# Row sums spread by VectorE transposes, the order of work in tables, and four LayerNorm tiles off TensorE

## The chip, the cores and the metric

The kernel runs on one core of one Trainium2 chip. A core has five engines with a queue of instructions each: TensorE (PE in the profile; its weight loads are the row PEld), VectorE (DVE), ScalarE (ACT), GpSimd (POOL) and SyncE (SP), which here only issues DMAs. Each queue runs in order; engines wait for one another by semaphores. The metric is the time of one execution on the device, in microseconds.

## The reference, cut to what matters

Eight sequences of 256 tokens with 512 features pass through four layers, all in float32: attention, a feed-forward layer, attention with other weights, and the same feed-forward layer again.

```python
x = x + _L0_attn_a_ref(_layernorm(x, axis=-1), w_qkv, w_o)
x = x + _L0_ffn_ref(_layernorm(x, axis=-1), gate_w, base_w, base_b, lora_A, lora_B)
x = x + _L0_attn_b_ref(_layernorm(x, axis=-1), wq, wk, wv, wo)
x = x + _L0_ffn_ref(_layernorm(x, axis=-1), gate_w, base_w, base_b, lora_A, lora_B)
```

Attention has 32 query heads on 8 key and value heads of 16 features, rotary embedding, a causal mask and a softmax. The feed-forward layer is a 512x512 projection with bias, plus low-rank terms of the two best of eight experts, weighted by a softmax over their two gate values.

## The kernel before, in words

The work is 16 units: a sequence in its first attention and feed-forward layer, or the same sequence in its second pair. Units 0 to 3 and 8 to 11 are first passes, 4 to 7 and 12 to 15 the second. A unit has two tiles of 128 tokens (t = 0, 1). For each tile a LayerNorm gives `xn` (statistics L631 to L635 and L638 on VectorE, a power L637 on GpSimd, the scaling L640 on ScalarE), four TensorE transposes (L647) turn it, and ScalarE copies the result out of PSUM (L654) into `xnT` or `yT`, features on partitions.

An attention unit then projects keys (L675), values (L686) and queries (L746), and applies the rotary embedding on VectorE and GpSimd from tables in `rtab`; the cosines and sines come by two DMAs on ScalarE's queue and two VectorE copies (L602). Scores are computed twice. The first pass (L801; groups s10 to s14) is copied to a `big` buffer (L816), masked by GpSimd (L832) and reduced to row maxima (L846), which a TensorE transpose (L855), a copy (L858) and DMAs put into spare rows of `q`. The second pass (L887; s20 to s24) gives transposed scores with the maximum taken off, which ScalarE exponentiates (L902) and GpSimd masks (L913). The value matmuls (L932; pv) sum them against `vp`, which also has 16 columns of ones for each group of four heads. So their PSUM result holds outputs and row sums interleaved: for half s, rows 32i to 32i+31 hold 16 rows of outputs and 16 equal rows of sums.

ScalarE copies this result to `e`, 128x2x512 (L947). Two DMAs gather the sums to `sums` (L952), VectorE takes the reciprocal of 128x32 (L955), two DMAs write it to DRAM as `recd` (L959), and one reads it back, each row repeated 16 times, as `rec` (L963). COPY_PREDICATED (L966) merges the two halves of `e`, overwriting sums, and a multiplication (L970) scales by `rec`. Then come the output projection (L978) and the addition to x (L985). The feed-forward layer has the gate and low-rank matmul (L999), the gate's small steps on VectorE (L1018 to L1044), a transpose (L1049), the 512x512 matmul (L1063), the low-rank matmul (L1069) and the addition (L1079).

Everything is registered with `plan.add(engine, cost, tag, function, reads, writes, ...)` before anything is issued: 2,955 operations. A planner, `Plan.schedule`, then walks through time with its own costs. For each engine it starts the ready operation with the lowest rank from the list `RANKS`, provided that its buffers are free; it lends PSUM banks and pooled buffers as it goes. The order in which it started them is the order of issue, so each engine's queue has it. TensorE's steps have a kind: full (128-row matmuls and transposes), score (L801, L887) and value (L932). SyncE has every load and store but the two tables; at most eight DMAs are under way.

The steps of the start that matter later: SyncE loads the first tile of sequence 0, its second tile, then the two halves of the first query weights (copied into place by VectorE, L556). The first full projection is L746 on both tiles.

Of the kernel before, what the change touches and what calls it, by code (L numbers as in the profile page):

```python
# [26 lines left out]
CHANGE = {"full": 0.08, "score": 0.16, "value": 0.13}  # L27
APART = 0.07
WINDOW = 3.4
SPLIT = 16  # L30
FIXED = 1.65
QUEUED = 8
# [3 lines left out]
RANKS = """  # L36
0 65 400 0 585 195 130 455 260 680 716 752 788 390 1870 955 2165 3555 325 3195 1105 1655 2615 2760
715 3645 1030 1795 2830 520 650 1240 1520 2905 1725 2255 2685 1280 1338 1680 1738 0 100 200 300 400
500 615 637 676 761 335 396 406 430 491 521 609 680 413 474 484 508 567 597 736 810 1676 1945 1852
2084 2150 2187 2277 2410 2345 2346 2373 2444 2566 2525 2657 2607 876 1407 1609 1674 1796 2515 1053  # L40
1230 1432 1497 1514 2150 3485 3130 2800 2922 3015 3259 3392 3532 3313 3435 3528 3779 3942 4228 4060
3741 3956 3863 4105 4216 4388 4514 4124 4411 4246 4565 4644 4743 4414 4779 4536 4977 5056 5142 5024
5235 5331 5266 5434 5644 5740 5675 5913 6035 6128 6237 6349 6203 6325 6418 6588 6797 6371 6511 6604
6527 6805 6712 6728 6991 6898 7100 7212 7105 7262 7371 7436 7710 7789 7854 8059 7571 8439 8920 9311
6914 7339 7550 7659 7724 8405 8450 8515 8735 8025 9203 9383 9931 9372 9654 9664 9893 9992 10057
10329 10400 11025 10882 11003 11037 11089 11072 11161 11301 11212 11456 11585 11672 11771 10472
12243 12372 10005 10066 10076 10428 10598 10683 10836 10907 11281 11560 11789 11823 11952 11858
11988 12039 12059 12079 12088 12347 12454 11075 12632 12824 1133 1194 1204 1228 1287 1317 1584 1655
824 885 895 919 978 1008 1630 1705 2038 2307 2214 2425 2723 2760 2642 3325 3260 2669 2811 2882 3271
3180 3312 3221 2897 3090 3353 3292 3525 3652 2446 2623 2872 2937 3005 3132 3870 3940 4927 5049 5142  # L50
5262 5522 5713 5229 5351 5444 5655 5766 6163 5995 5623 5745 5838 6004 6115 6522 6354 7487 7643 7736
7845 7924 8090 7237 7457 7364 7566 7645 7804 6620 6697 6728 6793 8328 8574 8605 8670 7781 7996 7903
8105 8371 10039 10254 10161 10480 10689 10978 11202 11109 11463 11585 11678 10375 10590 10497 11152
11436 11694 11859 11968 12033 12233 12405 12340 12610 12168 12990 13178 13600 11834 12009 12166
12470 12275 12670 12780 12715 13010 12698 13390 13590 13965 13829 13890 13900 14611 14932 14967
15090 15208 15067 15814 15935 15969 16021 16004 16057 16108 16128 16148 16157 16720 16763 15426
17193 17306 14026 14087 14097 14480 14539 14845 14947 15039 14933 16624 16745 16836 16947 16871
16983 17054 17034 17074 17083 17374 17411 16829 17479 17620 1055 1116 1126 1150 1211 1241 2400 2475
2794 2855 2865 2953 3059 3108 3267 3362 3472 4031 3648 4149 4302 4339 4327 4215 4280 4354 4423 4494
4872 4913 4679 4629 4573 4750 5025 4964 5135 5395 3838 4221 4449 4682 4723 4850 5594 5529 8080 8202  # L60
8295 9084 9217 9433 8177 8481 8388 8664 8846 9142 8974 8533 8655 8748 9782 10051 10832 10304 8823
9078 8985 9545 9624 9710 9286 9408 9501 9703 9945 10083 11451 11491 11702 11572 11439 11476 11507
11637 12141 12268 12361 12470 12582 12535 12750 12657 12859 13479 14993 15115 15258 14480 14752
14609 15329 15451 15544 15653 15765 14037 14248 14422 14357 14839 14884 14949 15154 14867 15534
17664 18055 16007 16198 16355 16529 16464 16737 16782 16847 17052 16765 17445 19336 19790 18116
18177 18187 18238 18362 18530 18943 19014 18655 19702 19823 19912 20106 20264 20213 20435 20308
20590 20599 22493 22549 20029 22630 23042 19851 20168 20178 20234 20295 20325 20681 20765 20415
20837 21048 21228 21309 21263 21493 21661 21681 21729 22387 22602 22720 21779 22754 22903 1898 1959
1969 1993 2052 2134 3410 3621 2998 3072 3082 4053 4289 4339 4511 4729 7589 7878 7987 8105 8311 8348
8344 8171 8236 10024 8525 8775 8853 8894 8935 9171 5052 5446 5648 5934 5877 8217 8356 8630 8848 8913  # L70
8957 9418 9617 9552 9749 9871 9964 10162 10295 10611 12829 13044 12951 13188 13368 13539 13661 13081
13330 13237 13883 14148 14434 14266 14185 14434 14341 14663 14742 14945 13940 14155 14062 14330
14532 14618 15790 15827 15858 15923 15802 15842 15988 16053 16330 16550 16457 16659 16771 18122
18244 18337 18446 18782 19895 20126 20219 16732 16854 16967 19798 20013 19920 20122 20286 19086
19297 19406 19471 20185 20230 20295 20500 19699 20880 22143 22660 20490 20949 21114 21223 21288
# [143 lines left out]
class Plan:  # L219

# [40 lines left out]
    def schedule(self, rank, limit):  # L269
# [36 lines left out]
        while done < len(ops):  # L306
# [71 lines left out]
            if not events:  # L378
                return None
# [772 lines left out]
```

## Time and profile before

| | us |
|---|---|
| three runs | 774.79, 775.36, 775.76 |
| median | 775.36 |
| the profiled execution | 773.26 |
| its span, first to last instruction | 771.6 |
| TensorE busy in it | 756.0 |
| VectorE, ScalarE, GpSimd busy | 505.9, 486.7, 513.6 |

TensorE's granted clock was 1.000 in the span. Busy time leaves out semaphores, branches and DMA issues. A line such as `A <- B: 26.7, 14, 6.6` in a view of waits says that A's engine sat idle before A until B ended, for 26.7 us in all, 14 times, at most 6.6 us. A group's line gives the operation, its operands by the program's names, its shape and count, then busy time, the mean of one in ns, and idle time before it. In a timeline the first two numbers are start and length.

### The profile page before, as it was taken

How to read it: one execution, taken by the hardware profiler on the slowest of the kernel's cores; microseconds unless marked ns; L12 is line 12 of the kernel's file. 1: busy time of each engine (PE TensorE's matmuls, PEld its weight loads, DVE VectorE, ACT ScalarE, POOL GpSimd, SP SyncE). 2: the span in 40 equal slices, each digit the busy share in tenths (PEclk: the TensorE clock that was granted, in tenths of full speed). 3: DMA queues.
4: the chain of work that ended last, by engine and by line, in shares of the span. 5: the costliest groups of instructions: out<-in, count | busy, mean ns of one | idle time of the engine just before them, and what ended most of it. 6: DMA issues, size and time to landing. Idle time of an engine off the chain costs nothing.

```text
span 771.6 us, 17960 instructions
## 1 busy us (share of the span) xinstructions
PE 756.0 (98%) x7196; PEld 410.9 (53%) x7196; DVE 505.9 (66%) x1035; ACT 486.7 (63%) x700; POOL 513.6 (67%) x495
## 2 busy tenths in 40 slices
PE   8999999999999999999999999999999989999998
PEld 7874555556456464555555465455555434544354
DVE  6574895856698358666557469465975894666564
ACT  4687757756666654685657566764576775657631
POOL 5898894848667586586738467696468974764530
PEclk9999999999999999999999999999999999999999
DMA  9820101101010020202021210020011100110111
GB/s 298 226 77 6 35 28 38 45 16 33 17 48 5 18 61 2 76 31 62 2 72 48 71 49 3 4 62 16 16 34 51 42 4 18 49 44 32 45 32 54
DMA packets 46755, 36.06 MB, mean 47 GB/s; under 512 B 28496, under 2 KB 31568, under 8 KB 46672
## 3 DMA queue, kind: packets, MB, share of 16 engines
q1 hardware_dynamic: 46128, 34.89, 15.0%
q8 instruction: 56, 0.92, 0.5%
q14 instruction: 27, 0.22, 0.1%
q10 hardware_dynamic: 544, 0.03, 0.0%
HBM read 19.71 MB, written 4.72 MB: 32 GB/s over the span
## 4 chain that ended last, share of the span: by engine, by line
PE 89%; DVE 4%; ACT 3%; issue 2%; POOL 2%; DMA 1%; SPq 0%; POOLq 0%; ACTq 0%; DVEq 0%
PE banks L746 14%; PE banks L1063 13%; PE banks L978 13%; PE banks L887 10%; PE banks L932 9%; PE banks L801 9%; PE banks L675 4%; PE banks L686 4%; PE banks L999 4%; PE banks L1069 4%; PE banks L647 3%; DVE nm L846 2%; POOL big L832 1%; ACT big L902 1%; ACT big L816 1%
## 5 line engine op out<-in xcount | busy, mean ns | idle before, releaser
L832 POOL TENSOR_SCALAR_AFFINE_SELECT big<-big 64x1024 f32<-64x1024 f32 (+1 forms) x160 | 172.4, 1078 | 72.3 <-ACT big L816 66.6
L846 DVE TENSOR_REDUCE nm<-big 128x8 f32<-128x1536 f32 (+3 forms) x112 | 184.7, 1670 | 36.3 <-POOL big L832 36.0
L913 POOL TENSOR_SCALAR_AFFINE_SELECT big<-big 64x1024 f32<-64x1024 f32 (+1 forms) x96 | 145.4, 1514 | 80.1 <-ACT big L902 74.9
L816 ACT COPY big<-banks 128x1024 f32<-128x1024 f32 (+1 forms) x164 | 154.9, 998 | 63.3 <-PE banks L801 60.6
L902 ACT ACTIVATE big<-banks 128x1024 f32<-128x1024 f32 (+1 forms) x166 | 156.6, 993 | 42.0 <-PE banks L887 40.7
L746 PE MATMUL banks<-xnT,wqkv 128*128 128x256 f32 x512 | 120.9, 384 | 1.0 <-ACT xnT L654 0.8
L1063 PE MATMUL banks<-base_sb,yT 128*128 128x512 f32 x256 | 117.4, 601 | 0.9 <-ACT big L902 0.7
L978 PE MATMUL banks<-wo,e 128*128 128x512 f32 x256 | 117.2, 601 | 0.4 <-ACT big L816 0.4
L746 PEld LDWEIGHTS banks<-xnT,wqkv 128*128 128x128 f32 x512 | 93.8, 190 | 29.5 <-issue 13.0
L887 PE MATMUL banks<-q,kz 32*64 32x512 f32 (+1 forms) x1536 | 91.7, 537 | 0.2 <-ACT big L902 0.2
L801 PE MATMUL banks<-kz,q 32*64 32x384 f32 (+3 forms) x2048 | 88.4, 442 | 1.8 <-ACT big L816 1.6
L932 PE MATMUL banks<-big,vp 64*32 64x512 f32 (+1 forms) x1536 | 77.2, 522 | 1.2 <-ACT big L902 1.2
L1063 PEld LDWEIGHTS banks<-base_sb,yT 128*128 128x128 f32 x256 | 46.1, 190 | 59.7 <-issue 48.1
L978 PEld LDWEIGHTS banks<-wo,e 128*128 128x128 f32 x256 | 46.4, 190 | 57.6 <-issue 50.8
L637 POOL TENSOR_TENSOR st<-st,neg_half 128x1 f32<-128x1 f32 x64 | 36.6, 573 | 55.1 <-DVE st L635 35.0
L640 ACT ACTIVATE xn<-x,st 128x512 f32<-128x512 f32 x64 | 52.1, 818 | 19.9 <-DVE st L638 19.6
L801 PEld LDWEIGHTS banks<-kz,q 32*64 32x64 f32 x2048 | 36.9, 130 | 42.1 <-issue 16.7
L932 PEld LDWEIGHTS banks<-big,vp 64*32 64x32 f32 x1536 | 26.8, 106 | 52.8 <-issue 37.0
L994 POOL TENSOR_TENSOR x<-x,bias_sb 128x512 f32<-128x512 f32 x32 | 40.6, 1271 | 18.6 <-ACT xn L640 17.3
L966 DVE COPY_PREDICATED e<-half_i,e 128x512 f32<-128x512 uint32 x32 | 33.1, 1036 | 29.9 <-DMA sums<-e 25.3
L766 POOL TENSOR_TENSOR ro<-ro,rtab 128x512 f32<-128x512 f32 x32 | 41.6, 1301 | 14.1 <-DVE ro L760 12.8
L970 DVE TENSOR_TENSOR e<-e,rec 128x512 f32<-128x512 f32 x32 | 32.7, 1021 | 26.7 <-DMA rec<-recd 26.7
(73 smaller groups left out, 877.6 us busy)
## 6 DMA issues: line engine op xcount, KB each, us to landing
q<-q SPq DMA_DIRECT2D x32, 256.0 KB
rec<-recd SPq DMA_DIRECT2D x32, 256.0 KB
x<-in_x SPq DMA_DIRECT2D x16, 256.0 KB
out<-x SPq DMA_DIRECT2D x16, 256.0 KB
big<-in_wqkv_a SPq DMA_DIRECT2D x2, 512.0 KB
wo<-in_wo_a SPq DMA_DIRECT2D x4, 256.0 KB
big<-in_wq_b SPq DMA_DIRECT2D x2, 512.0 KB
base_sb<-in_base_t SPq DMA_DIRECT2D x4, 256.0 KB
```

The costliest lines, as they stand in the source:

```text
L640: add("ACT", 0.82, (u, z + "ln"), lambda: nc.scalar.activation(at("xn", k), xt(b, t), AF.Identity, bias=st(10, 11), scale=st(9, 10)), [xk, ...
L746: nc.tensor.matmul(at("bank", k)[:, (j % 2) * S : (j % 2 + 1) * S], W[:, c, j * P : (j + 1) * P], xnT()[:, c, :], start=(c == 0), stop=(c ...
L801: nc.tensor.matmul(ps[64 * c : 64 * c + 64, base // 256 * 256 : base // 256 * 256 + 2 * dist] .rearrange("p (s k) -> p s k", s=2)[:, :, ba ...
L816: add("ACT", 1.03, (u, f"s1{gr}"), lambda h=h, kb=kb: [nc.scalar.copy(at("big", kb)[:, 2 * h + lo : 2 * h + hi, :], ps) for lo, hi, ps in ...
L832: nc.gpsimd.affine_select(out=v, in_=v, compare_op=ALU.is_ge, fill=MASKED, base=0, pattern=[[0, 2048 // w], [0, blocks * w // 2048], [-1, ...
L846: nc.vector.tensor_reduce(nmv(t)[:, :, m0 : m0 + k, :, g], v, AX.X, ALU.max, negate=True)
L887: nc.tensor.matmul(ps[64 * s : 64 * s + 64, 256 * col : 256 * (col + ng)], kz2()[lo : lo + 32, s, k * P + 64 * h : k * P + 64 * h + 64], q ...
L902: add("ACT", 1.03, (u, f"s2{gr}"), lambda z=z, kb=kb: [nc.scalar.activation(pv_(kb)[:, 2 * z + lo : 2 * z + hi], ps.rearrange("p z (g n) - ...
L913: nc.gpsimd.affine_select(out=v, in_=v, compare_op=ALU.is_ge, fill=0.0, base=0, pattern=[[0, 16 * nm], [1, 64]], channel_multiplier=-1,)
L932: nc.tensor.matmul(ps[s][32 * i : 32 * i + 32, 256 * g : 256 * (g + ng)].rearrange("p (g n) -> p g n", n=256), vp()[64 * s : 64 * s + 64, ...
L978: nc.tensor.matmul(at("bank", ("wo", km)), e()[:, 1, j * P : (j + 1) * P], WO[:, j, :], start=(j == 0), stop=(j == 3),)
L1063: nc.tensor.matmul(ps, at("yT", k)[:, c, :], base_sb[:, c, :], start=(c == 0), stop=False)
```

## The change

It has three parts.

1. The reciprocal of the row sums. The five DMAs, `sums` and `recd` go. For each half s VectorE transposes `e[:, s, :]` in 32x32 blocks into `rec`; in each block 16 columns now hold the sums, and a reciprocal of one column of each block, 16 in all, goes to `inv`. A third blockwise transpose reads `inv` with each element repeated 16 times and writes `rec` as before. Six operations of a tile become five, all on VectorE.
2. Four of 64 LayerNorm tiles, marked by ones in `TURNED` (place 4 x unit + 2 for the feed-forward layer + t): unit 8 attention t = 1, unit 10 attention t = 0, unit 13 attention t = 1, unit 14 feed-forward t = 0. Their `xn` is transposed in 32x32 blocks in place by VectorE, four DMAs write its 32-row strips to a DRAM buffer `scr` so that the blocks land transposed (rows of 128 bytes), and one DMA reads 512 rows of 512 bytes into `xnT` or `yT`. Their TensorE transposes and ScalarE copies go.
3. The planner, its costs and `RANKS` go. `TIMES` holds a number for each of the 2,939 operations in the order of registration, and sorting by it gives the order of issue; `LOANS` names the buffer that each operation takes. All engines' orders differ from those before.

In the table, the operations of the start are numbers 0 to 8 (loads on SyncE and, 2 and 3, of cosines and sines on ScalarE's queue), 9 to 12 (the copies of the query weights), 47 and 48 (the copies of cosines and sines), 49 (their transposes), 51 to 58 (LayerNorm of tile 0), 59 to 66 (of tile 1) and 83 (first query projection); 229 is a statistics step of unit 1. By their entries VectorE's queue begins 47, 51, 52, 53, 48, 9, 55, 59, 60, 61, 229, 63, 230, 10; before, it began 51, 52, 53, 59, 60, 61, 55, 63, 47, 48, 9 to 12. SyncE's loads begin with tile 0, the first half of the query weights, tile 1, a tile of unit 1, one of unit 8, and the second half of the query weights.

```diff
-CHANGE = {"full": 0.08, "score": 0.16, "value": 0.13}
...
+TURNED = "0000000000000000000000000000000001000000100000000000010000100000"
...
+TIMES = """
+0 1240 620 0 4340 620 3100 1860 5580 4500 7015 8050 8510 6200 4960 12170 19270 28210 29450 31930
+27590 9370 16470 12920 14420 46050 7440 17370 8060 6820 3720 34380 30690 32550 13670 15770 36210
+15800 18170 20020 23510 0 2000 3707 5307 6307 8420 2170 4050 4707 9175 3150 3760 3860 4100 4860 5160
+7307 8022 5250 5860 5960 6200 6785 7085 7960 8675 12960 15650 14720 16835 19210 19780 25880 17990
...
+LOANS = """
+4 2 0 3 2 4 0 1 2 2 7 1 0 1 5 2 1 0 0 3 0 0 1 14 21 2 3 28 1 0 0 7 14 3 3 38 2 28 10 4 5 0 6 1 5 11
...
     def run(self):
-        self.prepare()
-        rank = [int(z) / 100 for z in RANKS.split()]
-        best = self.schedule(rank, 1e9)
...
+        loans = iter([int(z) for z in LOANS.split()])
+        self.start = [int(z) / 1000 for z in TIMES.split()]
...
+        self.order = sorted(range(len(self.ops)), key=lambda n: (self.start[n], n))
...
+        "scr": tiles(64, [D, P], "scr", dram),
...
+    def turned(k):
+        return int(TURNED[4 * k[0] + 2 * (k[1] == "f") + k[2]])
...
+        way = turned(k)
+        if way != 0:
+            add("DVE", 0.70, (u, z + "lnT"), lambda: nc.vector.transpose(at("xn", k), at("xn", k)),
+                [], [kn])
+            for i in range(4):
+                add("SP", FIXED + 0.5, (u, z + "lnT"), lambda i=i: nc.sync.dma_start(
+                    at("scr", k).rearrange("(j a) (i b) -> i a j b", a=32, b=32)[i],
+                    at("xn", k)[32 * i : 32 * i + 32, :].rearrange("a (j b) -> a j b", b=32)),
...
+            add("SP", FIXED + 1.2, (u, z + "lnT"), lambda: nc.sync.dma_start(
+                dst(), at("scr", k).rearrange("(c p) n -> p c n", p=P)),
...
+        if way == 1:
+            return
...
-            sums, rec, recd = (lambda km=km, z=z: at("e", km)[z] for z in (1, 2, 3))
+
+
+            inv, rec = (lambda km=km, z=z: at("e", km)[z] for z in (1, 2))
             for s in range(2):
-                add("SP", FIXED + 0.1, (u, "e"), lambda s=s, e=e, sums=sums: nc.sync.dma_start(
...
-            add("DVE", 0.36, (u, "e"), lambda sums=sums: nc.vector.reciprocal(sums(), sums()),
...
+                add("DVE", 0.70, (u, "e"), lambda s=s, e=e, rec=rec: nc.vector.transpose(
+                    rec(), e()[:, s, :]), [(u, "e", t, s)], [(u, "rec", t)])
+                add("DVE", 0.25, (u, "e"), lambda s=s, rec=rec, inv=inv: nc.vector.reciprocal(
+                    inv()[:, :, s], rec().rearrange("p (j b) -> p j b", b=32)[:, :, 16 * (1 - s)]),
+                    [(u, "rec", t)], [(u, "inv", t, s)])
+            add("DVE", 0.70, (u, "e"), lambda rec=rec, inv=inv: nc.vector.transpose(
+                rec(), inv().unsqueeze(3).to_broadcast([P, 16, 2, 16])),
+                [(u, "inv", t, s) for s in range(2)], [(u, "rec", t)])
```

## The prediction

> **What bounds the kernel now.** I read the page first, then the busy time by stretch, then who waited for whom on TensorE and on VectorE, and last the timeline of the first 10 us. The page's engine row, and the chain that ended last:
>
> ```profile
> PE 756.0 (98%) x7196; PEld 410.9 (53%) x7196; DVE 505.9 (66%) x1035; ACT 486.7 (63%) x700; POOL 513.6 (67%) x495
> ...
> PE 89%; DVE 4%; ACT 3%; issue 2%; POOL 2%; DMA 1%; SPq 0%; POOLq 0%; ACTq 0%; DVEq 0%
> ```
>
> TensorE (PE) is busy 98% and carries 89% of the chain, so what counts is TensorE's own work and where it sits idle. By stretch:
>
> ```profile
> 0.00:20.00 20.00, 16.95 (x95) 15.24 (x96) 13.00 (x44) 7.92 (x11) 10.28 (x24) 1.00 0.91 294
> 20.00:600.00 580.00, 577.02 (x5627) 319.00 (x5626) 382.68 (x758) 381.38 (x547) 409.96 (x389) 1.00 0.14 42
> 600.00:645.00 45.00, 39.82 (x447) 18.99 (x446) 36.10 (x58) 33.19 (x48) 31.79 (x31) 1.00 0.06 20
> 645.00:771.00 126.00, 122.19 (x1032) 57.68 (x1031) 74.12 (x175) 64.22 (x95) 61.54 (x54) 1.00 0.13 41
> ```
>
> After the length come TensorE, weight loads, VectorE, ScalarE, GpSimd. From 20 to 600 us TensorE idles 3.0 of 580 us. A late start has no slack there to vanish in. The one loose stretch is 600 to 645 us, 5.2 us idle, with VectorE busy 36.1 of 45. The longest waits shown for TensorE itself are small, 11.5 us in all, 3.0 of them before its first projection:
>
> ```profile
> PE banks L1049 <- DVE gl L1044: 2.2, 1, 2.2
> PE banks L801 <- ACT big L816: 1.6, 2, 1.1
> ```
>
> None is for the reciprocal's path (sums, recd, rec). VectorE does wait for it:
>
> ```profile
> DVE e L970 <- DMA rec<-recd: 26.7, 14, 6.6
> DVE e L966 <- DMA sums<-e: 25.3, 8, 9.6
> ...
> DVE sums L955 <- DMA sums<-e: 14.7, 6, 4.5
> ```
>
> So the five DMAs cost 66.7 us of blocked VectorE, hidden from TensorE.
>
> **The reciprocal chain.** 32 tiles lose five DMAs (SyncE issue medians 0.616 for rec, twice 0.560 for sums, twice 0.547 for recd: 32 x 2.83 = 90.6 us of SyncE's queue) and one reciprocal of 0.341. The DMAs of q, vp and the row maxima queued behind those waits go out earlier; TensorE shows no wait on them, so I count nothing. Each tile gains three 128x512 transposes and two 16-column reciprocals. The trace has no transpose. Nearest is STREAM_SHUFFLE L760, 128x512 f32, 0.735; below lies the plain COPY L556, 0.42; above COPY_PREDICATED L966, mean 1.036. I take 0.735. The reciprocal lies between 0.164 (one column, L1030) and 0.341 (32 columns): 0.25. Per tile 3 x 0.735 + 2 x 0.25 - 0.341 = 2.36, times 32 = 75.6 us. With four transposes of the turned tiles (2.9) VectorE goes from 505.9 to 584 us, 76%; by the ends, 547 to 616. Blocked time of 66.7 us goes, so VectorE is occupied 78.5 - 66.7 = 11.8 us more. I do not expect transposes to wait for GpSimd: the SBUF-to-SBUF shuffle L700 runs 434 to 466 ns over 16 runs, while L970 runs 673 to 1694.
>
> The Trainium skill, "VectorE: DVE Perf Modes", section "The three transpose paths", gives 311 ns for a 128x128 bf16 transpose on VectorE, and its "Rules for kernel authors" advise TensorE for a full 128x128 transpose. Four times that would be, as an estimate, 1.24 us per 128x512 tile, and VectorE would go to some 634 us. That speaks against the change; the shuffle row speaks for the cheaper price, and no run here shows a transpose yet.
>
> **The four turned tiles.** TensorE loses 16 transposes of L647 (start to start 0.436 us per tile when a full matmul follows): -1.74 us. ScalarE loses four copies of 0.59. SyncE gains 20 issues of some 0.55, 11 us. The new path is 0.74 transpose, 4 x 0.55 issue, a landing, 0.6 issue and a landing of 2.9 (x<-in_x: issued 0.81, used 3.70; the writes are smaller, so I take 2.1): 8.5 us. In the table's order the TensorE work between transpose and first consumer is 11.9 us or more, so the path is hidden. Tightest is unit 14's feed-forward tile: two row-max DMAs of unit 13 stand between its writes and its read on SyncE, and the read lands about 1 us before the gate matmul. If that cover goes, TensorE waits 0 to 2 us; I take 0.
>
> **The order: changes of matmul kind.** A TensorE step takes longer when the next is of another kind (full, score, value), as start-to-start times show:
>
> ```profile
> 539.21 1.09 PE L999 MATMUL banks<-gl_sb,yT 128*128 128x136 f32 x8
> 540.23 1.11 PE L801 MATMUL banks<-kz,q 32*64 32x512 f32 x16
> 541.27 1.99 PE L675 MATMUL banks<-xnT,wqkv 128*128 128x256 f32 x8
> ...
> 556.92 1.09 PE L999 MATMUL banks<-gl_sb,yT 128*128 128x136 f32 x8
> 557.85 0.27 PE L855 MATMUL banks<-ident,nm 128*32 128x128 f32 x1
> ```
>
> L999 takes 1.02 before a score step and 0.93 before a full one: leaving full costs 0.094. Over the trace, leaving score costs 0.135 (1.044 against 0.909) and leaving value 0.164 (1.450 against 1.286). Counted along TensorE's order, full is left 136 times before and 148 by the new table, score 148 and 154, value 34 and 36: 12 x 0.094 + 6 x 0.135 + 2 x 0.164 = +2.27. With -1.74, TensorE's own work changes by **+0.5 us**.
>
> **The order: the start.** Now the cosine and sine copies (L602) stand behind both tiles' first steps; the table puts the cosine copy first on VectorE.
>
> ```profile
> 1.30 0.49 ACTq L563 DMA_DIRECT2D trig_tok<-in_cos  x1
> 3.70 0.69 DVE L631 BATCH_NORM_STATS2 st<-x 128x6 f32<-128x512 f32 x1 [1.69 <-DMA x<-in_x]
> 4.72 0.68 DVE L631 BATCH_NORM_STATS2 st<-x 128x6 f32<-128x512 f32 x1
> 6.47 0.21 DVE L638 TENSOR_SCALAR st<-st 128x1 f32<-128x1 f32 x1 [0.55 <-POOL st L637]
> 6.60 0.48 DVE L602 COPY rtab<-trig_tok 128x256 f32<-128x256 f32 x2
> 9.14 7.17 PE L746 MATMUL banks<-xnT,wqkv 128*128 128x256 f32 x32 [0.78 <-ACT xnT L654]
> ```
>
> Columns are start and length. The cosines are the second DMA of ScalarE's queue; the trace's semaphore counts complete them at 4.72 us, a microsecond after the first x tile is in use. VectorE runs in order, so all else waits behind that copy: copy to 5.05; tile 0's statistics to its epsilon step 1.10 (3.70 to 4.80) to 6.15; the sine copy and one weight permute (0.28 + 0.42) and the scale step to 7.07; tile 1's statistics 1.08 to 8.15; its scale step 0.67 + 0.05 later, with another batch's statistics in that gap, 8.87; ScalarE starts 0.25 later and takes 0.81, to 9.93; transposes and copy 1.34 (6.77 to 8.11 for tile 0) and 0.06 to the matmul: 11.33 against 9.14. **+2.2 us**. Low end: cosines landing with the sines, 3.90, +1.4; landed before x, only the copy and the other batch's statistics stand ahead, +1.1. High end: 0.5 MB of weights now follows on the queue where 0.25 MB of x did, and at 294 GB/s the difference is 0.85: +3.0.
>
> **The order: waits in mid-run.** For each TensorE step I compared the TensorE work between it and its producer with the durations between them: 30 steps before and 24 after have too little, short by 10.2 and 9.7 us. PSUM banks are reused within half a microsecond of their release 103 times before, 78 after. The overfull stretch around units 11, 13 and 14 keeps its shape. I take 0. Ends: all 8.5 us of mid-run waits vanish, or the 11.8 us of added VectorE occupancy all reaches TensorE.
>
> **Sum.** 2.2 + 0.5 + 0 = +2.7 us. The profiled execution took 773.26 us (span 771.6, 1.7 around it), 2.1 below the median of 775.36. It would become 775.96, span 774.3; for the median of runs, **778.1 us**.
>
> **Rivals.** *Waits shrink (faster):* the reordered chains and looser banks take most of the 8.5 us away. It decides from 2.7 us up, and past 0.2% from 4.3: 775.36 + 2.7 - 4.3 to 8.5 gives 773.8 down to 769.6. For it: 66.7 us of blocked VectorE gone. Against: TensorE waits on none of it. *VectorE becomes late:* half of 11.8 reaches TensorE, +5.9, 784. For it: at 36.1 of 45 us busy TensorE already lost 5.2. *The start does not bite:* the cosines land early or TensorE's feed catches up by 2.2: 775.9, no change.
>
> **Numbers.** This kernel's measurement tells about 0.2% (1.55 us) from no change. Forecast 0.40 (own range 775.5 to 780.5), waits shrink 0.26, VectorE late 0.20, start harmless 0.14. Faster gets 0.25 (nearly all of waits shrink); within 0.2% 0.22 (start harmless, the forecast's low edge); slower 0.53. The range of 8 in 10 leaves out the last part of waits shrink below 770.5 and of VectorE late above 784.5.
>
> **What would show it.** First L746 near 11.3 us, an L602 ending a DMA wait before the first L631; transposes near 0.735; VectorE near 584 us; kind changes 338, not 318; DMA waits of L966 and L970 gone; 600 to 645 us still loose. Wrong if L746 starts by 9.5, if transposes cost over 1 us or wait for GpSimd, or if TensorE's idle time after 20 us falls by more than 3 us.

## The result and the profile after

The changed kernel took 781.12 us (median of 4 runs, 780.19 to 782.08) beside 775.08 us for the kernel before (773.98 to 775.76): a ratio of 1.0066, 95% interval 1.0046 to 1.0086. The direction came out, the size did not: 0.66% where 778.1 us meant 0.35%. 781.12 lies inside the range of 8 in 10 (770.5 to 784.5) but above the forecast's own range (775.5 to 780.5), half-way to the rival in which VectorE becomes late (784). The profiled execution took 781.09 us, its span 779.4, so 7.8 us more than the profiled one of before.

From the page of the changed kernel: the span, the engines' busy times, and the chain that ended last.

```profile
span 779.4 us, 17973 instructions
...
PE 763.9 (98%) x7180; PEld 409.1 (52%) x7180; DVE 550.5 (71%) x1167; ACT 496.2 (64%) x858; POOL 507.1 (65%) x495
...
PE 72%; POOL 11%; DVE 7%; issue 5%; ACT 4%; DMA 1%; POOLq 0%; ACTq 0%; SPq 0%; DVEq 0%
```

TensorE is still busy 98%, and carries 72% of the chain where it carried 89%. VectorE gained 44.6 us, not the 78 predicted, and ScalarE gained 158 instructions, which the prediction did not mention. The same four stretches as before:

```profile
0.00:20.00 20.00, 15.74 (x77) 13.70 (x78) 10.72 (x39) 5.98 (x8) 6.80 (x18) 1.00 0.95 310
20.00:600.00 580.00, 576.77 (x5569) 314.12 (x5568) 413.66 (x850) 386.76 (x675) 399.81 (x388) 1.00 0.11 31
600.00:645.00 45.00, 41.80 (x432) 20.05 (x434) 38.03 (x65) 33.15 (x54) 38.01 (x35) 1.00 0.10 29
645.00:771.00 126.00, 125.10 (x1109) 59.57 (x1094) 84.75 (x204) 69.96 (x120) 62.52 (x56) 1.00 0.07 21
```

In the first 20 us TensorE is busy 15.74 us, where it was 16.95; from 20 to 600 us it idles 3.2 us, where it was 3.0; and 600 to 645 us, the loose stretch, idles 3.2 where it was 5.2. VectorE carries 31 us more from 20 to 600 us, and TensorE hardly shows it.

In VectorE's groups (count, busy us, mean ns, idle before) the new chain stands like this:

```profile
L896 DVE STREAM_TRANSPOSE rec<-e 128x512 f32<-128x512 f32 x64 | 45.2, 707 | 41.2 <-ACT e L889 40.4
...
L904 DVE COPY_PREDICATED e<-half_i,e 128x512 f32<-128x512 uint32 x32 | 29.4, 920 | 0.4
...
L901 DVE STREAM_TRANSPOSE rec<-inv 128x512 f32<-128x512 f32 x32 | 22.3, 701 | 0.6
...
L898 DVE RECIPROCAL inv<-rec 128x16 f32<-128x16 f32 x64 | 15.5, 244 | 0.8
```

A float32 transpose of 128x512 takes 0.70 us, a 16-column reciprocal 0.244. The DMA waits are gone from COPY_PREDICATED, but VectorE now stands 40.4 us before the first transpose, for ScalarE's copy of `e`: most of the blocked time changed its place.

The start, first from the timeline of the kernel before (start, length, then idle time before and what ended it):

```profile
1.43 4.56 PE L593 MATMUL banks<-ident 128*128 128x128 f32 x24 [1.43 <-POOL neg_half L502]
6.83 0.66 PE L647 MATMUL banks<-ident,xn 128*128 128x128 f32 x4 [0.84 <-ACT xn L640]
...
7.76 0.60 PE L647 MATMUL banks<-ident,xn 128*128 128x128 f32 x4
```

and from that of the changed kernel:

```profile
1.43 2.82 PE L512 MATMUL banks<-ident 128*128 128x128 f32 x12 [1.43 <-POOL neg_half L421]
...
5.74 0.29 DVE L521 COPY rtab<-trig_tok 128x256 f32<-128x256 f32 x1 [3.73 <-DMA trig_tok<-in_cos]
5.95 0.69 DVE L553 BATCH_NORM_STATS2 st<-x 128x6 f32<-128x512 f32 x1
...
6.09 0.69 PE L530 MATMUL banks<-ident,rtab 128*128 128x128 f32 x2 [1.84 <-DVE rtab L521]
...
7.78 1.92 PE L512 MATMUL banks<-ident 128*128 128x128 f32 x8
...
9.48 1.06 PE L589 MATMUL banks<-ident,xn 128*128 128x128 f32 x4
...
11.02 1.12 PE L589 MATMUL banks<-ident,xn 128*128 128x128 f32 x4 [0.47 <-ACT xn L562]
...
11.93 1.06 PE L512 MATMUL banks<-ident 128*128 128x128 f32 x4
...
12.81 3.74 PE L688 MATMUL banks<-xnT,wqkv 128*128 128x256 f32 x16
```

VectorE's first statistics start 2.25 us later than before (5.95 against 3.70), because the copy of the cosines heads its queue. Both sets of TensorE transposes take over 1 us, where before they took 0.60 to 0.66. The first query projection starts at 12.81 us, against 9.14.

L512 (L593 before) are 24 warm-up transposes of the identity matrix, six sets of four (numbers 41 to 46 of the table). Before, they run in one piece. The new order puts the tables' transposes (L530) behind the third set, where TensorE waits 1.84 us for the cosines, and the last set right before the projection.

**Where the 7.8 us are.** For each TensorE step I took the time to the start of the next one. The shortest that occurs before, for each step and the kind that follows it, counts as own work; everything above counts as wait, which includes work done at a lower clock. The few pairs that do not occur before have no such shortest time there, and grouping the steps a little differently moves a figure by up to 0.6 us and the differences by 0.3.

| us | own work | waits | first query projection | TensorE's end |
|---|---|---|---|---|
| before | 733.9 | 31.6 | 9.14 | 767.9 |
| after | 735.0 | 38.0 | 12.81 | 775.4 |
| after, another execution | 735.0 | 37.5 | 12.24 | 774.9 |

Of the 7.8 us, 3.7 lie before the first projection (nearly all of it waits). Of the waits behind that point, 28.1 became 30.9: 2.8. Own work is 1.1 more, and 0.2 come behind TensorE's end. The waits that grew lie at 300 to 400 us (2.0 to 3.8) and 500 to 600 us (1.7 to 4.1); those of 600 to 700 us fell from 9.4 to 7.4.

### The profile page after: what moved, and what is told of

Read it like the earlier page. It is cut to its first block, busy times and chain, and to the rows that moved or that the text cites. A ratio compares the mean times of both kernels' runs of the same rounds, so it can differ in the third digit from the quotient of the medians.

```text
span 779.4 us, 17973 instructions
## 1 busy us (share of the span) xinstructions
PE 763.9 (98%) x7180; PEld 409.1 (52%) x7180; DVE 550.5 (71%) x1167; ACT 496.2 (64%) x858; POOL 507.1 (65%) x495
## 4 chain that ended last, share of the span: by engine, by line
PE 72%; POOL 11%; DVE 7%; issue 5%; ACT 4%; DMA 1%; POOLq 0%; ACTq 0%; SPq 0%; DVEq 0%
PE banks L916 11%; PE banks L1001 10%; PE banks L688 10%; PE banks L829 9%; PE banks L874 9%; PE banks L743 6%; POOL big L774 6%; PE banks L1007 3%; DVE nm L788 3%; PE banks L937 3%; PE banks L589 3%; PE banks L628 3%; PE banks L617 3%; POOL ro L708 1%; ACT big L844 1%
## 5 line engine op out<-in xcount | busy, mean ns | idle before, releaser
L774 POOL TENSOR_SCALAR_AFFINE_SELECT big<-big 64x1024 f32<-64x1024 f32 (+1 forms) x160 | 168.5, 1054 | 76.5 <-ACT big L758 65.6
L758 ACT COPY big<-banks 128x512 f32<-128x512 f32 (+1 forms) x245 | 160.9, 727 | 60.5 <-PE banks L743 56.3
L844 ACT ACTIVATE big<-banks 128x512 f32<-128x512 f32 (+1 forms) x236 | 162.3, 753 | 49.1 <-PE banks L829 46.7
L855 POOL TENSOR_SCALAR_AFFINE_SELECT big<-big 64x1024 f32<-64x1024 f32 (+1 forms) x96 | 142.0, 1480 | 71.3 <-ACT big L844 62.3
L688 PE MATMUL banks<-xnT,wqkv 128*128 128x256 f32 x512 | 123.3, 387 | 0.2 <-ACT big L758 0.2
L829 PE MATMUL banks<-q,kz 32*64 32x512 f32 (+1 forms) x1536 | 93.4, 537 | 0.9 <-DMA q<-nmT 0.3
L896 DVE STREAM_TRANSPOSE rec<-e 128x512 f32<-128x512 f32 x64 | 45.2, 707 | 41.2 <-ACT e L889 40.4
L553 DVE BATCH_NORM_STATS2 st<-x 128x6 f32<-128x512 f32 x64 | 43.8, 687 | 6.6 <-DMA x<-in_x 5.7
L829 PEld LDWEIGHTS banks<-q,kz 32*64 32x64 f32 x1536 | 27.0, 130 | 35.5 <-issue 16.9
```

Source lines behind the costliest of these rows:

```text
L688: nc.tensor.matmul(at("bank", k)[:, (j % 2) * S : (j % 2 + 1) * S], W[:, c, j * P : (j + 1) * P], xnT()[:, c, :], start=(c == 0), stop=(c ...
L758: add("ACT", 1.03, (u, f"s1{gr}"), lambda h=h, kb=kb: [nc.scalar.copy(at("big", kb)[:, 2 * h + lo : 2 * h + hi, :], ps) for lo, hi, ps in ...
L774: nc.gpsimd.affine_select(out=v, in_=v, compare_op=ALU.is_ge, fill=MASKED, base=0, pattern=[[0, 2048 // w], [0, blocks * w // 2048], [-1, ...
L829: nc.tensor.matmul(ps[64 * s : 64 * s + 64, 256 * col : 256 * (col + ng)], kz2()[lo : lo + 32, s, k * P + 64 * h : k * P + 64 * h + 64], q ...
L844: add("ACT", 1.03, (u, f"s2{gr}"), lambda z=z, kb=kb: [nc.scalar.activation(pv_(kb)[:, 2 * z + lo : 2 * z + hi], ps.rearrange("p z (g n) - ...
L855: nc.gpsimd.affine_select(out=v, in_=v, compare_op=ALU.is_ge, fill=0.0, base=0, pattern=[[0, 16 * nm], [1, 64]], channel_multiplier=-1,)
```

## The experiments

Ratios are to the kernel before on the same chip, with 95% intervals.

### 1. The start: the copies of the tables, then the whole start

In e1, against the changed kernel, the copies of cosines and sines (47 and 48), their transposes (49) and another unit's statistics (229, 230) go behind the first steps of tile 0:

```diff
...
-15800 18170 20020 23510 0 2000 3707 5307 6307 8420 2170 4050 4707 9175 3150 3760 3860 4100 4860 5160
+15800 18170 20020 23510 0 2000 3707 5307 6307 8420 6790 6795 7965 9175 3150 3760 3860 4100 4860 5160
...
-116732 117252 117082 117607 118317 118117 118517 118607 121642 122017 112412 132352 133487 6030 6915
+116732 117252 117082 117607 118317 118117 118517 118607 121642 122017 112412 132352 133487 6800 6920
```

> The changed kernel with one thing undone at the start: the copies of cosines and sines stand behind both tiles' first LayerNorm steps again (VectorE: 51, 52, 53, 9, 55, 59, 60, 61, 63, 47, 48, 229, ...), and their TensorE transposes behind the tiles' own. Theory (the late first projection is lost for good): the first L688 falls from 12.81 us to about 9.8, since the second x tile lands about a microsecond later than before, and the execution is 3.0 us shorter than the changed kernel's. Rival (the rest of the chain catches up): the first L688 is early, but the time falls by under 1 us, because later waits on loads or on the tables take it back.

Measured: 780.39 us, ratio 1.0068 (1.0046 to 1.0091); span 777.9 against 779.4. The first projection started at 11.49 us, 1.32 earlier, and TensorE's last step 1.45 earlier. The gain is within what the timed runs can tell; the trace shows it passed to the end in full. Theory had asked for 9.8 us and a gain of 3.0. In this trace TensorE waits 1.51 us for the second tile's `xn`, and its granted clock is then 0.50 from 9.1 to 12.5 us, while the tables' transposes and the last four warm-up transposes still stand ahead of the projection. That is 1.7 us of lost clock (0.5 x 3.41), about what the gain lacks.

In e5 SyncE's loads stand as before as well (tile 0, tile 1, then the query weights), and the weights' copies behind the two tables; the last set of warm-up transposes (46) moves forward from 8420 to 7000, so that all six run ahead of the first tile's. Numbers 229 and 230 are as in e1, and one later load moves back a little:

```diff
-0 1240 620 0 4340 620 3100 1860 5580 4500 7015 8050 8510 6200 4960 12170 19270 28210 29450 31930
+0 620 620 0 3705 1240 1860 2480 5580 6792 6793 6794 6795 6200 4960 12170 19270 28210 29450 31930
...
-15800 18170 20020 23510 0 2000 3707 5307 6307 8420 2170 4050 4707 9175 3150 3760 3860 4100 4860 5160
+15800 18170 20020 23510 0 2000 3707 5307 6307 7000 6790 6791 7700 9175 3150 3760 3860 4100 4860 5160
```

> The changed kernel with its whole start as before: both tiles of sequence 0 loaded ahead of the query weights, the copies of cosines and sines behind the tiles' first steps, their transposes between the tiles' transposes, the permutes right behind; nothing else moved. Theory (all of the start's loss is order, and all of it counts): first L688 at 9.2 us, not 12.81, the last TensorE step 3.6 us earlier, span about 775.8. Rival (part of the loss is caught up): the last TensorE step at most 2 us earlier.

Measured: 778.17 us, ratio 1.0035 (1.0022 to 1.0048), half of the change's loss. From the timeline of this kernel:

```profile
3.71 0.69 DVE L553 BATCH_NORM_STATS2 st<-x 128x6 f32<-128x512 f32 x1 [1.70 <-DMA x<-in_x]
...
6.67 0.66 PE L589 MATMUL banks<-ident,xn 128*128 128x128 f32 x4 [0.37 <-ACT xn L562]
...
8.56 0.65 PE L589 MATMUL banks<-ident,xn 128*128 128x128 f32 x4
...
9.89 1.16 PEld L688 LDWEIGHTS banks<-xnT,wqkv 128*128 128x128 f32 x6 [0.91 <-ACT xnT L596]
```

The statistics start where they did before, the transposes take 0.66 us again, and the projection starts at 9.89: 2.9 us earlier than in the changed kernel, with TensorE's end 3.0 earlier. A microsecond lost ahead of the first projection is lost at the end. 9.2 us and a gain of 3.6 had been expected; the 0.75 us that are left against the kernel before begin with the second tile's statistics, which start at 5.68 instead of 4.72 us, behind a step of the first tile that waits for GpSimd.

### 2. Banks in pairs

The planner tried to give adjacent PSUM banks to operations that fill two; `LOANS` has 172 that are apart (10 before), and ScalarE then evacuates in two instructions of 0.60 us instead of one of 1.02. In e2 only `LOANS` differs from the changed kernel's; 17 pairs are apart:

```diff
-4 2 0 3 2 4 0 1 2 2 7 1 0 1 5 2 1 0 0 3 0 0 1 14 21 2 3 28 1 0 0 7 14 3 3 38 2 28 10 4 5 0 6 1 5 11
+4 2 0 3 2 4 0 1 2 2 2 1 0 1 3 3 1 0 0 2 0 1 1 19 37 2 3 10 55 0 0 55 37 3 10 37 2 10 37 4 7 0 0 1 55
...
```

> The changed kernel with its order as it is and the PSUM banks lent anew, so that the two banks of a pair are neighbours: 17 pairs apart, not 172. ScalarE's evacuations in two halves become single ones, and ScalarE's instructions go from 858 to about 703. Theory (splits are ScalarE's own cost, some 0.07 us each, and hidden): ScalarE's busy time falls by about 11 us, TensorE's waits after the first projection by under 1 us. Rival (the added 2.8 us of mid-run waits come from late evacuations): 2 to 3 us faster than the changed kernel.

Measured: 781.55 us, ratio 1.0077 (1.0045 to 1.0109). ScalarE fell from 496.2 to 487.0 us busy, TensorE's waits went from 38.0 to 38.8. The split evacuations cost ScalarE 9 us and the kernel nothing.

### 3. The chain alone, in the order of before

e3 is the kernel before, with its order and buffers written into tables, and the new chain's five operations in VectorE's queue right ahead of their COPY_PREDICATED. No tile is turned.

```diff
-            add("DVE", 0.36, (u, "e"), lambda sums=sums: nc.vector.reciprocal(sums(), sums()),
...
+                    rec(), e()[:, s, :]), [(u, "e", t, s)], [(u, "rec", t)])
...
```

> The kernel before with its own order and buffers written into tables, no tile turned, and the reciprocal chain alone changed: the three transposes and two reciprocals stand on VectorE right before the COPY_PREDICATED. Theory (TensorE sees neither the DMAs that go nor the VectorE time that comes): within 1.5 us of the kernel before, VectorE busy at about 550 us. Rival (VectorE becomes late): 3 to 6 us slower, with TensorE waiting for row maxima, gates and LayerNorm steps. Second rival (blocked VectorE held TensorE after all): 2 us or more faster.

Measured: 790.88 us, ratio 1.0199 (1.0164 to 1.0233), three times the loss of the whole change and far over the rival's 3 to 6 us. Own work stayed at 733.9 us, waits rose from 31.6 to 49.8. TensorE's waits before, and in this kernel:

```profile
PE banks L647 <- ACT xn L640: 1.6, 3, 0.8
...
PE banks L855 <- DVE nm L846: 0.9, 2, 0.5
```

```profile
PE banks L830 <- DVE nm L821: 7.0, 7, 3.6
PE banks L622 <- ACT xn L595: 3.7, 4, 1.8
```

Its transposes of row maxima wait 7.0 us for VectorE's reductions, where it was 0.9, and its LayerNorm transposes 3.7 us for `xn`, where it was 1.6 (ScalarE waits for VectorE's statistics there). The largest place is this, from the timeline (TensorE first, then VectorE):

```profile
81.11 1.98 PE L776 MATMUL banks<-kz,q 32*64 32x256 f32 x64
86.65 0.37 PE L830 MATMUL banks<-ident,nm 128*32 128x128 f32 x1 [3.56 <-DVE nm L821]
86.82 3.62 PE L721 MATMUL banks<-xnT,wqkv 128*128 128x256 f32 x8
...
80.04 0.70 DVE L929 STREAM_TRANSPOSE rec<-e 128x512 f32<-128x512 f32 x1
...
82.10 0.71 DVE L934 STREAM_TRANSPOSE rec<-inv 128x512 f32<-128x512 f32 x1
82.73 1.61 DVE L937 COPY_PREDICATED e<-half_i,e 128x512 f32<-128x512 uint32 x1
84.24 2.27 DVE L821 TENSOR_REDUCE nm<-big 128x8 f32<-128x2048 f32 x1
```

The chain begins at 80.04, the reduction only at 84.24, and TensorE waits 3.56 us for it. So VectorE's queue does reach TensorE, against the prediction's step, once the order isn't made for it.

e4 is e3 with eleven LayerNorm tiles turned:

```diff
-TURNED = "0000000000000000000000000000000000000000000000000000000000000000"
+TURNED = "0000000110001000101000000000001000000000100010001000110000000000"
```

> The kernel of e3_chain with eleven LayerNorm tiles turned off TensorE, those whose consumer comes at least 12 us after the TensorE transpose in the old order. Theory (a turned tile saves TensorE its 0.44 us and nothing else is late): 11 x 0.44 = 4.8 us faster than e3_chain. Rival (VectorE's transpose and five more DMAs on SyncE's queue make other steps late): 0 to 2 us faster, or slower, with waits of TensorE on DMAs of q or on xnT and yT.

Measured: 797.25 us, ratio 1.0288 (1.0241 to 1.0334). Own work fell by 5.0 us to 728.9, waits rose by 11.6 to 61.4. Taking transposes off TensorE shortens its work by 0.45 us a tile, as predicted, and does not help here: the rival came.

### 4. The chain at a fraction of its time

e6 is the changed kernel with transposes and reciprocals of a sixteenth of the columns; e7 is the same edit on e3:

```diff
-                    rec(), e()[:, s, :]), [(u, "e", t, s)], [(u, "rec", t)])
+                    rec()[:, 0:32], e()[:, s, 0:32]), [(u, "e", t, s)], [(u, "rec", t)])
...
-                    inv()[:, :, s], rec().rearrange("p (j b) -> p j b", b=32)[:, :, 16 * (1 - s)]),
+                    inv()[:, 0:1, s], rec()[:, 16 * (1 - s) : 16 * (1 - s) + 1]),
...
-                rec(), inv().unsqueeze(3).to_broadcast([P, 16, 2, 16])),
+                rec()[:, 0:32], inv()[:, 0:1].unsqueeze(3).to_broadcast([P, 1, 2, 16])),
```

> The changed kernel with the chain's VectorE work nearly taken away: transposes over 32 of 512 columns and reciprocals of one column, the order unchanged; rec holds ones elsewhere, so outputs are not divided by their row sums. Theory (VectorE's added time is what TensorE waits for after the start): TensorE's waits after the first projection fall from 30.9 us to 28 or less, span 776.5 or less. Rival (the new order itself brings the waits): they stay within 1 us, span 778.5 to 779.4.

Measured: 779.61 us, ratio 1.0055 (1.0039 to 1.007), span 777.5, VectorE 504.6 us busy instead of 550.5. The first projection started 0.57 us earlier than in the changed kernel's profile; the waits behind it are 1.3 us less (29.6). That lies between the theory (28 or less) and the rival (within 1 us).

> The kernel of e3_chain with the same cheap chain (32 of 512 columns, reciprocals of one column, outputs not divided by their row sums). Theory (the 18 us of e3_chain are VectorE's time): back to the kernel before, span 770 to 773. Rival (it is where the five operations stand in VectorE's queue, waiting for ScalarE's copy of e, whatever their length): over 780. Third: if the DMAs that VectorE waited for had held TensorE, the span falls under 770.

Measured: 776.25 us, ratio 1.0006 (0.9997 to 1.0016), span 773.2, waits 33.2 us.

Two things follow. With the five DMAs gone and a short chain in their place (VectorE still 20 us busier than before, 526.3 against 505.9), the old order runs nearly as before, with 1.6 us more of waits: no cost of the DMAs to TensorE shows. And the same 46 to 47 us of VectorE's time cost TensorE 16.6 us of waits in the old order (e3 against e7: 49.8 and 33.2) but 1.3 in the new one. The new order is what lets the chain in; it costs some 1.5 us of waits by itself (2.8 less 1.3), and 2.8 of own work (e9, below).

### 5. The turned tiles

e8 is the kernel before with its order as tables and its DMA chain. Four tiles (18, 40, 44, 53) are turned, and ScalarE copies the turned cosines and sines behind the second tile's transposes:

```diff
-TURNED = "0000000000000000000000000000000000000000000000000000000000000000"
+TURNED = "0000000000000000001000000000000000000000100010000000010000000000"
```

> The kernel before with its old reciprocal chain and its own order in tables, two edits: four LayerNorm tiles with at least 15 us between TensorE's transpose and the consumer are turned (unit 4 feed-forward t = 0, unit 10 attention t = 0, unit 11 attention t = 0, unit 13 attention t = 1), and at the start ScalarE copies the cosine table behind the second xnT. Theory (with that much room a turned tile is worth its TensorE time): 4 x 0.45 + 0.4 = 2.2 us faster than the kernel before. Rival (VectorE's in-order wait for xn, and five DMAs more, come out as waits): within 0.5 us of it, or slower.

Measured: 778.5 us, ratio 1.0041 (1.0027 to 1.0055): the rival. The profiled execution was the slowest of five, 780.65 us. In it own work fell by 1.9 us, waits rose by 9.0. Not all of the 9 belongs to the tiles: 0.5 lie ahead of the first projection, where the second edit is, and some are lost clock, below.

e9 is the changed kernel with no tile turned. (Its expectation numbers the four tiles as in e8; in the changed kernel they are 33, 40, 53 and 58.)

```diff
-TURNED = "0000000000000000000000000000000001000000100000000000010000100000"
+TURNED = "0000000000000000000000000000000000000000000000000000000000000000"
```

> The changed kernel's order, buffers and chain on VectorE, but no LayerNorm tile turned on VectorE: the four tiles (18, 40, 44 and 53) are transposed on TensorE again, four matrices of 128x128 each, with their copy out of the banks on ScalarE, at places in the list near where their two DMAs stood. Theory (a turned tile is worth its transposes and costs nothing more in the new order): TensorE's own work rises by the 1.7 us that the prediction gave (16 steps of 0.109 us), its waits stay near 38 us, and the kernel takes about 1.7 us longer than the changed one: a ratio near 1.009. Rival (a tile turned on VectorE and carried by DMA comes late for its first matmul or holds VectorE from other work, as it did in the old order, where four cost 9 us of waits and saved 1.9): the waits fall by 2 to 9 us, and the kernel is 0 to 7 us faster than the changed one: a ratio of 0.998 to 1.007.

> The changed kernel itself, on the same chip as the run without turned tiles, so that the two stand against one base. Every theory expects its ratio near 1.0066 again, a span near 779.4 us, and TensorE's waits near 38 us.

Measured: without turned tiles 782.11 us, ratio 1.0089 (1.006 to 1.0117); the changed kernel 780.56, ratio 1.0072 (1.0045 to 1.0098). The spans are 780.4 and 778.8, own work 736.7 and 735.0, waits 37.6 and 37.5. The timed difference of 1.55 us is inside the intervals; the traces split it: the four tiles save TensorE 1.7 us of own work, and its waits are the same with and without them.

### 6. One chain moved, and all chains moved

e10 is e3 with one chain and its COPY_PREDICATED behind the next row-max reduction, whose entry is 809000:

```diff
...
-757093 757094 757095 757100 843900 892000 931100 691400 733900 755000 802491 802492 802493 802494
-802495 802500 920300 938300 993100 937200 965400 966400 989300 999200 1005700 1032900 1040000
+757093 757094 757095 757100 843900 892000 931100 691400 733900 755000 809001 809002 809003 809004
+809005 809006 920300 938300 993100 937200 965400 966400 989300 999200 1005700 1032900 1040000
...
```

> The kernel before's order with the new chain on VectorE (the run that took a ratio of 1.0199, span 789.8 us), and one thing changed in it: one of the 32 chains, that of unit 0's second tile (three transposes, two reciprocals and the COPY_PREDICATED, 80.0 to 84.2 us there), goes behind the row-max reduction that followed it. In that run TensorE waited 3.56 us for this reduction, and from 87 to 90 us its granted clock was 0.50, from 90 to 95 us 0.77. Theory (a wait that long costs its own length and then a slower clock): both go, 3.0 us of the wait and (0.26 x 3 + 0.50 x 3 + 0.23 x 5 =) 3.4 us of lost clock, so the span falls by 6 to 7 us to about 783.4, with the clock at 1.00 from 84 to 95 us, a ratio near 1.012. Rival 1 (a wait costs its own length only): the span falls by 3, ratio near 1.016. Rival 2 (VectorE's time comes back at the next place, whichever comes first): no change, ratio near 1.020.

Measured: 785.25 us, ratio 1.0134 (1.0117 to 1.0151), span 784.6. In its timeline the same place reads:

```profile
83.41 0.29 PE L830 MATMUL banks<-ident,nm 128*32 128x128 f32 x1 [0.32 <-ACT big L791]
83.54 1.89 PE L721 MATMUL banks<-xnT,wqkv 128*128 128x256 f32 x8
```

The transpose starts 3.24 us earlier, and the eight matmuls behind it take 1.89 us instead of 3.62. The windows of e3 (length, five engines, granted clock, DMA):

```profile
84.00:87.00 3.00, 0.35 (x2) 0.38 (x3) 3.00 (x5) 2.10 (x3) 1.60 (x2) 0.74 0.09 9
87.00:90.00 3.00, 3.00 (x9) 2.19 (x7) 1.31 (x2) 0.26 (x1) 2.98 (x3) 0.50 0.02 5
90.00:95.00 5.00, 5.00 (x58) 2.55 (x56) 0.54 (x2) 2.58 (x4) 1.19 (x2) 0.77 0.01 3
```

and of e10:

```profile
84.00:87.00 3.00, 3.00 (x42) 2.05 (x41) 2.93 (x8) 2.71 (x5) 1.78 (x3) 1.00 0.12 14
87.00:90.00 3.00, 3.00 (x25) 1.51 (x24) 1.97 (x4) 2.05 (x4) 2.93 (x4) 1.00 0.02 5
90.00:95.00 5.00, 5.00 (x26) 1.77 (x25) 4.33 (x5) 3.81 (x6) 4.85 (x4) 1.00 0.00 0
```

TensorE works through 87 to 95 us in both, at half the clock in the first. At the next pair of projections e10 is 5.9 us ahead (86.41 against 92.31), of which 5.2 reach the span: somewhat under the theory's 6 to 7, well over the 3 of a wait that costs only its length.

e11 is e3 with all 32 chains and their COPY_PREDICATED just before their multiplication (843900 and 920300 for the first two):

```diff
...
-651100 660400 652700 680500 671200 672800 699100 689800 710000 721200 710500 726200 757091 757092
-757093 757094 757095 757100 843900 892000 931100 691400 733900 755000 802491 802492 802493 802494
-802495 802500 920300 938300 993100 937200 965400 966400 989300 999200 1005700 1032900 1040000
+651100 660400 652700 680500 671200 672800 699100 689800 710000 721200 710500 726200 843892 843893
+843894 843895 843896 843897 843900 892000 931100 691400 733900 755000 920292 920293 920294 920295
+920296 920297 920300 938300 993100 937200 965400 966400 989300 999200 1005700 1032900 1040000
...
```

> The kernel before's order with the new chain on VectorE, all 32 chains with their COPY_PREDICATED moved as late on VectorE's queue as they can go, to just before their multiplication (0 to 17 VectorE operations later), past row-max reductions and LayerNorm steps. VectorE does the same work. Theory (the place of the chain in VectorE's queue decides, and there it stood ahead of work that TensorE waited for): most of the 18 us of added waits go, a ratio of 1.003 to 1.010. Rival 1 (VectorE's added time as such comes through wherever it stands): the ratio stays at 1.015 to 1.020. Rival 2 (late chains hold up the output projection instead): waits of that projection on the multiplication appear, and the ratio stays above 1.010 with TensorE idle there.

Measured: 838.64 us, ratio 1.0823 (1.0797 to 1.0849). TensorE's waits in its profile:

```profile
PE banks L949 <- DVE e L941: 27.4, 14, 3.1
PE banks L949 <- DVE gs L989: 4.0, 1, 4.0
```

The theory's number fell, Rival 2 came, far larger than I had expected: the output projection (L949) waits for the late multiplication. Waits rose to 97.4 us, with a mean granted clock of 0.975 over 837.4 us, which is 21 us of lost clock. The broad claim holds all the same, and stronger: with the same operations on every engine the kernel takes 785 us, 791 or 839 by the place of the 32 chains in VectorE's queue alone, and 782 in the new order (e9), where every engine's order differs.

No version tried is faster than the kernel before.

## Why the prediction was right or wrong

- **The start (+2.2, bounds +1.1 to +3.0): the place right, the size too small, even for the bounds.** It measured +3.7 in the profiled execution and +3.1 in another. Two terms failed. "The cosines complete at 4.72 us" was read from a start in which 0.25 MB of x shared the queues; with 0.5 MB of weights there they complete at 5.71 by the same semaphore counts (5.60 in the other execution), and at 4.66 in e5, where the loads stand as before. The prediction had this as its high end (0.85); it is 1.0. And "transposes and copy 1.34" carried over the durations of before, while the second tile's four transposes took 1.12 us instead of 0.60: some 0.5. With the 2.2 that makes 3.7. The prediction did not look at the warm-up transposes, which the new order splits; what that does to the clock stands in the last section. In the other execution, with sets of 0.85 and 0.66, the projection started 0.57 earlier.
- **That it has no slack to vanish in: right.** e5 gave back 2.9 us at the start and 3.0 at the end.
- **Kind changes (+2.27): 2.8 measured**, own work without turned tiles (736.7) less that of before (733.9).
- **Turned tiles (-1.74, path hidden): right in the new order** (736.7 to 735.0, waits unchanged). The tight tile of unit 14 shows no wait of its consumer above 0.2 us.
- **Mid-run waits (0): +2.8 measured**, 1.3 for the chain's time on VectorE and 1.5 for the order. It lay inside the bounds.
- **"Blocked time of 66.7 us goes, so VectorE is occupied 11.8 us more", and 11.8 as the upper end: the step that was wrong in kind.** Idle time was treated as a store from which the new work could be paid. It is not: VectorE still has to stand until ScalarE's copy of `e` is there (40.4 us now), and the operations then come in one piece (2.8 us in e3's lines above) ahead of whatever is queued. In e3 16.6 to 18.2 us reached TensorE, in e11 66. That 1.3 and not 16 us reached TensorE in the changed kernel is due to the order, which the prediction had no argument for; on this term it was lucky. Its comparison of work between producer and consumer said that the two orders were much alike (30 and 24 tight steps), but it weighed them with durations and didn't follow VectorE's queue with the chains in it.
- **Transposes 0.735, reciprocal 0.25: 0.70 and 0.244.** The estimate of 1.24 us per tile from the Trainium skill's "VectorE: DVE Perf Modes" ("The three transpose paths") is too dear for float32 at this size (0.70 measured); the shuffle row was the better neighbour.
- **VectorE at 584 us: 550.5.** The chain's groups came as priced (83.0 us for its transposes and reciprocals), but five groups that were not changed became shorter, 112.6 to 95.7 us together: COPY_PREDICATED (mean 1036 to 920 ns), the multiplication (1021 to 885) and three small gate operations. Why is open. Another 11.6 us are only a matter of counting: where neighbouring instructions overlap, busy time counts them once, and these overlaps rose from 37.7 to 49.3 us over the trace. (The stated upper end, 616, leaves out the turned tiles; with four at 1.036 it is 620.)
- **DMAs hidden: right, as far as e7 shows** (1.0006). **Waits shrink: did not happen**, the waits behind the first projection grew. **VectorE becomes late: its mechanism is real** (e3) and was averted by the order, 1.3 us instead of 5.9.
- **"600 to 645 us keeps its shape": nearly.** TensorE idles 3.2 us there instead of 5.2; 300 to 400 and 500 to 600 us lost more than that.
- **Overlooked:** the 162 more split evacuations. They cost nothing (e2), but nothing in the prediction could have said so.
- **The frame:** the two profiled executions differ by 7.8 us, the medians by 6.0, since the profiled one of before lies 1.8 under its median. Its granted clock was 1.000. On the chip of e9 the kernel before took 773.28 us at a clock of 1.000 and 781.12 at 0.991, in 12 executions, while the changed kernel stayed between 779.87 (1.000) and 782.72 (0.995): the kernel before loses clock in many of its executions, which narrows the difference of the medians.

## What to carry to other kernels

On an in-order queue the place of an operation decided more than its length here: look for what stands behind it in the queue and which engine waits for that, and don't count time in which an engine is blocked as room for new work. Ahead of the first full-size work of the bounding engine every microsecond counts, and TensorE's pace there depends on whether its early work runs in one piece. Taking hidden DMAs away was worth nothing by itself here; what replaces them must be found a place.

## What the hardware showed

**A wait of TensorE can cost about twice its length, because the granted clock falls behind it.** In e3 the wait of 3.56 us was followed by a clock of 0.74, 0.50 and 0.77 over 3, 3 and 5 us: (0.26 x 3 + 0.50 x 3 + 0.23 x 5) 3.4 us lost. Shorter waits can do it too. In e8 a wait of 2.24 us (L1030 for the gate's VectorE steps) was enough:

```profile
635.00:640.00 5.00, 2.76 (x26) 1.02 (x33) 4.83 (x10) 3.58 (x5) 3.88 (x3) 0.85 0.00 0
640.00:645.00 5.00, 5.00 (x39) 0.98 (x31) 1.93 (x7) 2.00 (x3) 1.29 (x2) 0.50 0.02 3
```

and the same wait in the kernel before, also 2.24 us, was not:

```profile
630.00:635.00 5.00, 2.76 (x34) 0.96 (x33) 4.80 (x10) 3.53 (x5) 3.81 (x3) 1.00 0.00 0
635.00:640.00 5.00, 5.00 (x78) 1.84 (x70) 2.31 (x8) 3.77 (x6) 1.78 (x3) 1.00 0.02 3
```

The traces' own records of the granted clock tell the two apart. In each of the fourteen traces the clock changes only at multiples of 3.413 us from its first record, and every spell at 0.50 while TensorE works lasts 3.41 us (12 of them) or 6.83 us (6). What counts is how much TensorE idles, by the profile's busy time, within one such slot of 3.413 us. Of some 3,140 slots at full clock, all 13 with more than 1.88 us idle were followed by a clock of 0.50, none with less than 1.38 was, and of the 14 between 5 were. In e8 the wait put 1.9 us of idle time into the slot from 635.1 to 638.5 us; in the kernel before a border at 633.0 us cut the same wait into 1.5 and 0.7. So where the borders fall decides about waits of this length. In e10 1.78 us in one slot was enough, and a wait of 2.09 us in e11, cut by a border, was not.

The Trainium skill, "TensorE: Matmul & The Clock Gate", section "Part 1: The HAM clock gate (the "warmup" mystery)", says that an idle window of about 3.4 us halves the clock. The depth, 0.50, and the length of a slot agree; but none of these slots held more than 3.02 us of idle time, and in e3 the clock fell at 85.5 us, while the wait was still on, behind a slot with 2.4 us of idle time.

So 3.4 of e8's 9 us of waits (0.5 x 6.83) follow a wait that was there before and are no cost of its turned tiles; another 1.7 (0.5 x 3.41) follow a wait of 1.38 us that was not. Likewise 5.1 us of e3's added 18 are lost clock (0.5 x 10.24). The profiled executions of the changed kernel and the one before have no such spell.

**TensorE's first work can be slow while the windows show a granted clock of 1.00.** In the changed kernel, after waits of 1.84 and 0.52 us for the tables, sets of four 128x128 transposes took 1.06 to 1.12 us up to 12 us into the run, in e5 and before 0.60 to 0.66, and the rows give 1.00 for all of them. The records of the clock begin at 5.0 us before and at 5.6 in e5, where the warm-up transposes run in one piece, but at 12.9 us in the changed kernel (9.9 in the other execution); a window counts time without a record as 1.00. Ahead of that point four transposes take 0.85 us from start to start in all of these traces, behind it 0.44 to 0.49. So the slow pace lasts until the first record, and a broken start makes it last longer: in the nine traces in which at least 20 of the 24 warm-up transposes run in one piece the records begin at 4.2 to 7.1 us, in the five in which they are split at 9.5 to 12.9.
